# Order of the first transfers, index loads on GpSimd's queue, and products of zeros ahead of the first data

## Chip, core and metric

The kernel runs on one core of one Trainium2 chip. The metric is device time in microseconds; the time before is the median of three runs. A profile is one execution, with its own time.

## The reference

There are 1024 tokens of 512 features (8 batches of 128) in fp32, and two layers.

- Layer 0: `x + ffn0(cond0(x))`. `cond0` is a gated feed-forward part, `down(silu(gate(x)) * up(x))`, with 1376 hidden features, in which each of gate, up and down has a low-rank addition `0.5 * B_b (A_b x)` of rank 16. The pair `A_b`, `B_b` is chosen per batch by an index (`itok_B_2_6`). `ffn0` is a gated feed-forward part of 1792 hidden features with weights `w * (su @ sv)`, where `su @ sv` has rank 4.
- Layer 1: `x + ffn1(cond1(x))`. `cond1` is one 512x512 product with bias and a low-rank addition chosen by a second index; `ffn1` is a gated part with group-scaled integer weights.

Everything the change touches belongs to the start of `cond0`.

## The kernel before

Features lie on the 128 partitions and tokens along the free dimension. x is four tiles `x[0..3]` of 128 features by 1024 tokens, each loaded in two halves of 512 tokens (`load_x`, line 103; 256 KB a half). `cond0` runs over eleven units of 128 hidden features. Per unit there is one weight tile `wgu` (gate and up, 512 KB) and one `wd` (down, 256 KB).

Gate and up of a unit are not computed with eight block products but with seven (a Strassen-like scheme): product 1 takes the tokens' first half and features 0 to 255 ("11"), product 2 the features 256 to 511 of the first half ("21"), product 3 those of the second half ("22"), and products 4 to 7 take sums of blocks, `T1` to `T4` on the token side (`token_forms`, line 240, on VectorE) and `s` on the weight side (`weight_forms`, line 233). Each product is four matmuls of 128x128 by 128x512. In the first unit the order is 1, 3, 2, 6 (`T2`), 7 (`T3`), 5 (`T1`), 4 (`T4`) (`gate_up`, line 341). `T3` = second half of features 256 to 511 minus second half of 0 to 255, `T1` = second minus first half of features 0 to 255, and `T2` is made from `T1`, so all three need second halves of x.

The low-rank additions need the batch indices. `index_tiles` (line 92) loads them twice, spread over 128 partitions by 8 batches and as one number per partition; `row_indices` (line 111) turns them into row numbers, and GpSimd gathers rows of the A and B tables by them: `gather_b` one transfer (`gb`), `gather_a` eight (`ga`), of which five can be in flight, each copied into place by GpSimd (line 177). `arrange_b` (line 546) then copies `gb` inside the on-chip memory into `b_rows4` with eight DMAs. In the second unit, after its products 1, 6, 7 and 5, TensorE computes the low-rank products (`pt_gu`, line 554) and with `b_rows4` the additions of both units (line 574).

What sets the order: matmuls, and a part of the other operations, are kept in program order (`in_order`, line 68); the rest is placed by a scheduler when the program is built. A DMA waits on the queue of the engine that issues it (SP, ACT or GpSimd), so later issues on that queue, and for ACT and GpSimd also its computing, stand behind it. In the old kernel the index loads of layer 0 are first on ACT's queue (line 99), then x0 to x3, first halves; on SP's queue are w0 in two parts of 256 KB (line 273), the second halves of x from x3 to x0, then layer 1's indices, w1, the first `wd`, `fs` (line 533, the rank-4 factors of `ffn0`), w2 to w4 and the copies for `b_rows4`.

PSUM is one pool of eight banks (`bank`, line 88) here.

Of the kernel before, what the change touches and what calls it, by code (L numbers as in the profile page):

```python
# [7 lines left out]
F32 = mybir.dt.float32  # L8
# [3 lines left out]
ALU = mybir.AluOpType  # L12

P = 128
# [4 lines left out]
G = 32  # L19
NG = P // G  # L20
TG = T // NG
H = 512
KC = H // P
# [6 lines left out]
RS = 4  # L30
CA = 2 * KC + NF0
B_WIDTH = 2 * F0P + H
AHEAD = 3
QBUFS = 10
LAG = 2


@with_exitstack
def kernel(
# [25 lines left out]
    nc = tc.nc  # L65

    nc_mm = nc.tensor.matmul
    in_order = tc.keep_in_program_order

    def mm(*args, **kwargs):  # L70
        in_order(nc_mm(*args, **kwargs))  # L71

    def pool(stack, name: str, side: str, bufs: int = 1):
        return stack.enter_context(
            tc.tile_pool(name=name, side=side, bufs=bufs, reuse_waits="tile")
        )

    const = pool(ctx, "const", "left")
    scales = pool(ctx, "scales", "left", 3)
# [8 lines left out]
    def bank(name: str):  # L88
        return psum.tile([P, TB], F32, tag="bank", name=name)


    def index_tiles(which: str, engine, idx: bass.AP, idx_rows: bass.AP):
        a = const.tile([P, NB], I32, tag=f"a_{which}", name=f"a_{which}")
        engine.dma_start(out=a, in_=idx.to_broadcast([P, NB]))
        b = const.tile([P, 1], I32, tag=f"b_{which}", name=f"b_{which}")
        engine.dma_start(out=b, in_=idx_rows)
        return a, b

    ix0 = index_tiles("0", nc.scalar, idx0, idx0_rows)

    x = [const.tile([P, T], F32, tag=f"x{k}", name=f"x{k}") for k in range(KC)]

    def load_x(engine, k: int, tb: int):
        engine.dma_start(out=x[k][:, bass.ts(tb, TB)], in_=xT[:, k, bass.ts(tb, TB)])
# [3 lines left out]
    rank = const.tile([P, 1], I32, tag="rank", name="rank")  # L108
    nc.vector.tensor_single_scalar(rank, partition[:, 0:1], R - 1, ALU.bitwise_and)

    def row_indices(which: str, ix):
        rows = []
        for name, of, times, plus in (("a", ix[0], P, partition), ("b", ix[1], R, rank)):
            to = const.tile(
                list(of.shape), I32, tag=f"{name}_rows_{which}", name=f"{name}_rows_{which}"
            )
            in_order(
                nc.vector.scalar_tensor_tensor(to, of, times, plus, op0=ALU.mult, op1=ALU.add)
            )
            rows.append(to)  # L120
        return rows

    a0_rows, b0_rows = row_indices("0", ix0)
    row_batch = const.tile([P, 1], I32, tag="row_batch", name="row_batch")
    nc.vector.tensor_single_scalar(row_batch, partition[:, 0:1], R * (NB // NTB - 1), ALU.bitwise_and)

# [135 lines left out]
    def product(ps, a, b, start: bool, stop: bool):  # L262
        for n, (w, src) in enumerate(zip(a, b)):
            mm(ps, w, src, start=start and n == 0, stop=stop and n == len(b) - 1)


    ready = {}

    def load_c(f: int):
        wgu = wgu_pool.tile([P, 2, KC, P], F32, tag="wgu", name=f"wgu_c{f}")  # L270
        if f == 0:
            for s in range(2):
                nc.sync.dma_start(out=wgu[:, s], in_=c_gu[f, :, s])
        else:
            nc.sync.dma_start(out=wgu, in_=c_gu[f])
        wd = wd_pool.tile([P, H], F32, tag="wd", name=f"wd_c{f}")
        ready["c", f] = wgu, wd
# [16 lines left out]
    def finish_c(f: int):  # L294
        gate_up_forms("c", f, nc.vector if f < 3 else nc.gpsimd)

    fs = const.tile([P, 3, H], F32, tag="fs", name="fs")

    def load_f(f: int):
        wgu = wgu_pool.tile([P, 2, KC, P], F32, tag="wgu", name=f"wgu_f{f}")  # L300
        nc.sync.dma_start(out=wgu, in_=f_gu[f])
        wd = wd_pool.tile([P, H], F32, tag="wd", name=f"wd_f{f}")
        nc.sync.dma_start(out=wd, in_=f_down[f])
        si = scales.tile([P, 3, P], F32, tag="si", name=f"si_{f}")
        for s in range(3):
            nc.sync.dma_start(out=si[s * G : s * G + RS, s], in_=f_si[f, :, s])
        ready["f", f] = wgu, wd, si

    def finish_f(f: int):
        wgu, wd, si = ready["f", f]  # L310

        pw = [bank(f"pw_{f}_{s}") for s in range(3)]
        for k in range(KC):
            for s in range(3):
                rows, ks = slice(s * G, s * G + RS), bass.ts(k, P)
                sv, su = fs[rows, s, ks], si[rows, s, :]
                mm(pw[s][:, ks], *((su, sv) if s == 2 else (sv, su)), start=True, stop=True)
        for s in range(2):
            nc.vector.tensor_tensor(
                wgu[:, s].rearrange("p k f -> p (k f)"),  # L320
                wgu[:, s].rearrange("p k f -> p (k f)"), pw[s], ALU.mult,
            )
        nc.vector.tensor_tensor(wd, wd, pw[2], ALU.mult)
        gate_up_forms("f", f, nc.gpsimd)

    units = [("c", f) for f in range(NF0)] + [("f", f) for f in range(NF)]
    load = {"c": load_c, "f": load_f}
    finish = {"c": finish_c, "f": finish_f}

# [11 lines left out]
    def gate_up(  # L341
        act_pool, temps, layer: str, f: int, b, adapters=None, first=False, last=False, between=None
    ):


        a = ready[layer, f][0]
        mul = (nc.vector if last else nc.gpsimd).tensor_tensor

        def temp(what: str):
            return temps.tile([P, TB], F32, tag=what, name=f"{what}_{layer}{f}", bufs=2)  # L350

        def new(i: int):
            return bank(f"p{i}_{layer}{f}")

        act = [act_pool.tile([P, TB], F32, tag="act", name=f"act_{layer}{f}_{tb}") for tb in range(2)]
        add = nc.vector.tensor_tensor
        done = adapters is None
        p1, u, v = temp("p1"), temp("u"), temp("v")
        ps = {}

        def of(i: int, src: str, stop: bool = True):
            ps[i] = new(i)
            product(ps[i], a[i], b[src], True, stop)
            return ps[i]

        nc.scalar.copy(p1, of(1, "11"))
        if first:
            of(3, "22", done)
            of(2, "21", done)
        add(u, of(6, "T2"), p1, ALU.add)  # L370
        add(v, of(7, "T3"), u, ALU.add)
        add(act[1], of(5, "T1"), v, ALU.add)
        add(u, ps[5], u, ALU.add)
        if between is not None:
            between()
        if not first:
            of(3, "22", done)
            of(2, "21", done)
        of(4, "T4", done)
        x2, x3, x4 = ps[2], ps[3], ps[4]  # L380

        def finish():
            if adapters is not None:
                x8 = new(8)
                adapters([[x2, x3], [x4, x8]], {(1, 1)})
            add(p1, x2, p1, ALU.add)
            nc.scalar.activation(p1, p1, AF.Silu)  # L387
            add(act[0], x4, v, ALU.add)
            mul(act[0], act[0], p1, ALU.mult)  # L389
            add(u, x3, u, ALU.add)  # L390
            nc.scalar.activation(u, u, AF.Silu)  # L391
            if adapters is not None:
                add(act[1], x8, act[1], ALU.add)
            mul(act[1], act[1], u, ALU.mult)  # L394

        for tb in range(NTB):
            acts[f, tb] = act[tb]
        return finish
# [112 lines left out]
    with ExitStack() as c_layer:  # L511
# [2 lines left out]
        xf, top = ExitStack(), ExitStack()  # L514
        x_forms = pool(xf, "x_forms", "left")
        temps = pool(top, "temps_c", "right")
        load_x(nc.scalar, 0, 0)
        load_c(0)
        for k in range(1, KC):
            load_x(nc.scalar, k, 0)  # L520
        for k in reversed(range(KC)):
            load_x(nc.sync, k, 1)
        finish_c(0)
        b_x = token_forms(x_forms, "x", x, True)
        b0 = gather_b(temps, "0", c_b, b0_rows, B_WIDTH)
        a0, a0_down = gather_a(temps, "0", c_a, a0_rows, [(temps, 2 * KC), (l0, NF0)], nc.gpsimd)
        b0_down = l0.tile([P, H], F32, tag="b0_down", name="b0_down")
        in_order(nc.gpsimd.tensor_copy(b0_down, b0[:, 2 * F0P :]))
        a1_rows, b1_rows = row_indices("1", index_tiles("1", nc.sync, idx1, idx1_rows))
        load_c(1)  # L530
        load_c_down(0)
        for s in range(3):
            nc.sync.dma_start(out=fs[s * G : s * G + RS, s], in_=f_s[:, s])
        load_c(2)
        finish_c(1)

# [109 lines left out]
    for sign in (1, -1):  # L646
        in_order(
            nc.gpsimd.affine_select(
                out=one, in_=one, pattern=[[-sign, P]], compare_op=ALU.is_ge,
# [38 lines left out]
    def load_q(f: int):  # L688
        wgu = l1.tile([P, 2, KC, P], F32R, tag="wgu_q", name=f"wgu_q{f}", bufs=QBUFS)
        nc.gpsimd.dma_start(out=wgu, in_=q_gu[f])  # L690
        wd = l1.tile([P, H], F32R, tag="wd_q", name=f"wd_q{f}", bufs=QBUFS)
        nc.gpsimd.dma_start(out=wd, in_=q_down[f])
        ready["q", f] = wgu, wd

    for f in range(QBUFS):
        load_q(f)
# [145 lines left out]
    for f in range(NF - 1):  # L842
        d = f - LAG
        if d > 0 and d - 1 + QBUFS < NF:
            load_q(d - 1 + QBUFS)
        gate_or_up(f, 0, 0)
# [41 lines left out]
    f = NF - 1  # L888
    for tb, at in enumerate(halves):
        d = f - LAG + tb  # L890
        for s in range(2):
# [131 lines left out]
```

## Time and profile before

| What | us |
|---|---|
| Median of three runs (731.67 to 737.83) | 733.24 |
| The profiled execution's own time | 732.24 |
| Its span, first to last instruction | 730.5 |
| TensorE busy (96% of the span) | 698.1 |
| GpSimd busy | 380.3 |
| VectorE busy | 364.8 |
| ScalarE busy | 152.4 |
| First matmul starts at | 8.35 |

Times in the profile count from the span's start. L71 is the one line that all matmuls of layer 0 go through (`mm`), so they are told apart by their tiles: `p_c` are the gate and up products of `cond0`, `pt_gu` the low-rank ones. PE is TensorE, PEld its weight loads, DVE VectorE, ACT ScalarE, POOL GpSimd; SPq, ACTq and POOLq are DMA issues of these engines. q1 is the queue of SP's DMAs, q10 of ACT's, q0 of GpSimd's.

### The profile page before, as it was taken

Reading aid. Unit: us, or ns where it says so; the run is one execution under the profiler, and the core shown is the slowest. Engines: PE = TensorE matmul, PEld = TensorE weight load, DVE = VectorE, ACT = ScalarE, POOL = GpSimd, SP = SyncE. Lnnn points to the kernel's source line nnn. Section 1 sums busy time; section 2 is a strip of 40 time slices with the busy share of each in tenths; the row PEclk is TensorE's granted clock in tenths of the full one; section 3 lists DMA queues with packets and bytes.
Section 4 is the critical chain, followed back from the end, with each engine's and each line's share of the span. In section 5 each row is a group of like instructions: output and inputs, shape, how many; then the busy total and the mean of one; then the engine's idle time right before and its main releaser. Section 6 shows DMA issues by size and latency. Waiting matters only on the chain.

```text
span 730.5 us, 6906 instructions
## 1 busy us (share of the span) xinstructions
PE 698.1 (96%) x2526; PEld 366.3 (50%) x2526; DVE 364.8 (50%) x478; ACT 152.4 (21%) x191; POOL 380.3 (52%) x353
## 2 busy tenths in 40 slices
PE   5999999999999999999999998799999899999993
PEld 2444444444344444444444443344436687788862
DVE  4544434434035555544545360423124798899974
ACT  1111101111000111111111110000014555656552
POOL 4543524437460253443443369851301798898885
PEclk9999999999999999999999999799999999999998
DMA  8951001110020221110200020000900130000003
GB/s 303 269 190 58 29 30 57 30 30 31 0 72 1 86 59 29 41 49 29 59 5 1 15 73 0 0 29 29 373 1 9 50 86 16 15 0 1 0 1 115
DMA packets 16341, 41.48 MB, mean 57 GB/s; under 512 B 2882, under 2 KB 3162, under 8 KB 16052
## 3 DMA queue, kind: packets, MB, share of 16 engines
q1 hardware_dynamic: 10548, 25.51, 11.3%
q0 software_dynamic: 4896, 14.49, 6.2%
q10 hardware_dynamic: 864, 1.05, 0.4%
q8 instruction: 20, 0.33, 0.2%
q14 instruction: 13, 0.11, 0.0%
HBM read 37.50 MB, written 2.10 MB: 54 GB/s over the span
## 4 chain that ended last, share of the span: by engine, by line
PE 77%; POOL 11%; DMA 5%; issue 3%; ACT 1%; DVE 1%; POOLq 0%; ACTq 0%; SPq 0%; DVEq 0%
PE p_f L71 22%; PE p_c L71 17%; PE d_c L71 10%; PE gu_q L757 9%; PE d_f L71 8%; PE d_q L757 4%; PE l L722 4%; POOL sum L772 3%; PE pw L71 2%; POOL x L772 2%; POOL act_lo L772 1%; DMA wgu_c<-in_c_gu_dram 1%; DMA b<-in_idx_rows_dram 1%; DMA b_rows<-gb 1%; DMA x<-in_xT_dram 1%
## 5 line engine op out<-in xcount | busy, mean ns | idle before, releaser
L766 DVE SCALAR_TENSOR_TENSOR sum<-gu_q,sg,sum 128x1024 f32<-128x1024 f32 (+1 forms) x75 | 90.6, 1211 | 22.6 <-ACT sum L763 18.7
L757 PE MATMUL gu_q<-h_hi,wgu_q 128*128 128x512 f32 x224 | 88.8, 396 | 3.0 <-ACT sum L763 2.0
L757 PE MATMUL gu_q<-h_lo,wgu_q 128*128 128x512 f32 x224 | 87.3, 390 | 0.0
L394 POOL TENSOR_TENSOR act_f<-act_f,u_f 128x512 f32<-128x512 f32 x13 | 16.5, 1271 | 79.2 <-ACT u_f L391 79.2
L772 POOL TENSOR_TENSOR sum<-sum,sum 128x1024 f32<-128x1024 f32 (+1 forms) x15 | 33.9, 2258 | 38.7 <-DVE sum L766 38.7
L71 PE MATMUL p_f<-h,wgu_f 128*128 128x512 f32 x112 | 53.9, 603 | 0.0
L766 DVE SCALAR_TENSOR_TENSOR x<-d_q,sd,x 128x1024 f32<-128x1024 f32 (+1 forms) x49 | 53.0, 1100 | 0.9 <-PE d_q L757 0.9
L71 PE MATMUL p_f<-T_h,s_f 128*128 128x512 f32 x112 | 52.6, 592 | 0.0
L71 PE MATMUL p_f<-T_h,wgu_f 128*128 128x512 f32 x112 | 52.6, 592 | 0.0
L71 PE MATMUL p_c<-x,wgu_c 128*128 128x512 f32 x88 | 44.2, 626 | 8.3 <-DMA x<-in_xT_dram 8.3
L763 ACT ACTIVATE sum<-gu_q,sg 128x1024 f32<-128x1024 f32 (+1 forms) x45 | 47.3, 1056 | 20.0 <-PE gu_q L757 20.0
L757 PEld LDWEIGHTS gu_q<-h_hi,wgu_q 128*128 128x128 f32 x224 | 42.0, 188 | 17.3 <-ACT sum L763 3.0
L389 POOL TENSOR_TENSOR act_c<-act_c,p_c 128x512 f32<-128x512 f32 x10 | 12.8, 1277 | 70.3 <-ACT p_c L387 70.3
L757 PE MATMUL d_q<-act_hi,wd_q 128*128 128x512 f32 x112 | 44.7, 399 | 2.9 <-ACT y L763 1.6
L71 PE MATMUL d_f<-act_f,ds_f 128*128 128x512 f32 x84 | 40.2, 632 | 6.7 <-POOL ds_f L238 6.7
L757 PEld LDWEIGHTS gu_q<-h_lo,wgu_q 128*128 128x128 f32 x224 | 42.1, 188 | 8.2
L757 PE MATMUL d_q<-act_lo,wd_q 128*128 128x512 f32 x112 | 43.8, 391 | 0.8 <-POOL act_lo L772 0.8
L772 POOL TENSOR_TENSOR act_lo<-sum,act_hi 128x1024 fp32r<-128x1024 f32 (+1 forms) x15 | 33.8, 2255 | 17.8 <-ACT act_hi L833 17.8
L71 PE MATMUL p_c<-T_x,wgu_c 128*128 128x512 f32 x88 | 41.3, 592 | 0.0
L71 PE MATMUL p_c<-T_x,s_c 128*128 128x512 f32 x88 | 41.3, 592 | 0.0
L772 POOL TENSOR_TENSOR x<-x,y 128x1024 f32<-128x1024 f32 (+1 forms) x19 | 36.6, 1940 | 0.0
L71 PE MATMUL d_f<-act_f,wd_f 128*128 128x512 f32 x84 | 36.4, 592 | 0.0
(163 smaller groups left out, 1119.3 us busy)
## 6 DMA issues: line engine op xcount, KB each, us to landing
wgu_f<-in_f_gu_dram SPq DMA_DIRECT2D x14, 512.0 KB
wgu_q<-in_q_gu_dram POOLq DMA_DIRECT2D x14, 512.0 KB, 6.0
wgu_c<-in_c_gu_dram SPq DMA_DIRECT2D x10, 512.0 KB
wd_f<-in_f_down_dram SPq DMA_DIRECT2D x14, 256.0 KB
wd_q<-in_q_down_dram POOLq DMA_DIRECT2D x14, 256.0 KB
wd_c<-in_c_down_dram SPq DMA_DIRECT2D x11, 256.0 KB
out_dram<-x SPq DMA_DIRECT2D x8, 256.0 KB
b_rows<-gb SPq DMA_DIRECT2D x8, 176.0 KB
```

The source lines that it names most:

```text
L71: in_order(nc_mm(*args, **kwargs))
L389: mul(act[0], act[0], p1, ALU.mult)
L394: mul(act[1], act[1], u, ALU.mult)
L722: nc.tensor.matmul(l_sums[o][:, tb], lw[:, k, bass.ts(o, P)], x[k][:, bass.ts(tb, TB)], start=(k == 0), stop=False,)
L757: nc.tensor.matmul(ps, w, part[:, at], start=(n == 0), stop=(n == len(src) - 1))
L763: in_order(nc.scalar.activation(to, ps, AF.Identity, scale=scale))
L766: nc.vector.scalar_tensor_tensor(to, ps, scale, plus, op0=ALU.mult, op1=ALU.add)
L772: in_order(nc.gpsimd.tensor_tensor(to, a, b, op))
```

## The change

- The loads of layer 0's indices go from ACT's queue to GpSimd's, and the row numbers are computed on GpSimd, each with two operations (multiply, add) instead of one on VectorE. Layer 1's stay on SP's queue and on VectorE, with two operations each.
- w0 is loaded in four parts of 128 KB. The parts of w0 and the eight halves of x are laid on the queues of SP and ACT in the order of the products: SP gets w0 gate first part, x1, w0 gate second part, w0 up in two parts, then the second halves of x3 and x1; ACT gets x0, x2, x3 and then the second halves of x2 and x0.
- In the first unit product 2 comes before product 3.
- `fs` becomes one tile of 128x512 instead of 128x3x512. It is set to zero by VectorE at the start, and TensorE multiplies these zeros by each other four times (`WARM`) into a bank that nobody reads. The rank-4 factors are loaded over it later, the three factors on different partitions; `si` is cut in the same way.

```diff
+WARM = 4
...
+    fs = const.tile([P, H], F32, tag="fs", name="fs")
...
-    ix0 = index_tiles("0", nc.scalar, idx0, idx0_rows)
+    in_order(nc.vector.memset(fs, 0.0))
+    warm_bank = bank("warm")
+    for _ in range(WARM):
+        mm(warm_bank, fs[:, :P], fs, start=True, stop=True)
+
+    ix0 = index_tiles("0", nc.gpsimd, idx0, idx0_rows)
...
-            in_order(
-                nc.vector.scalar_tensor_tensor(to, of, times, plus, op0=ALU.mult, op1=ALU.add)
-            )
+            in_order(engine.tensor_single_scalar(to, of, times, ALU.mult))
+            in_order(engine.tensor_tensor(to, to, plus if name == "a" else plus[:, 0:1], ALU.add))
...
-        if f == 0:
-            for s in range(2):
-                nc.sync.dma_start(out=wgu[:, s], in_=c_gu[f, :, s])
-        else:
+        if f:
             nc.sync.dma_start(out=wgu, in_=c_gu[f])
...
-        si = scales.tile([P, 3, P], F32, tag="si", name=f"si_{f}")
+        si = scales.tile([P, P], F32, tag="si", name=f"si_{f}")
         for s in range(3):
-            nc.sync.dma_start(out=si[s * G : s * G + RS, s], in_=f_si[f, :, s])
+            nc.sync.dma_start(out=si[s * G : s * G + RS], in_=f_si[f, :, s])
...
         if first:
+            of(2, "21", done)
             of(3, "22", done)
-            of(2, "21", done)
...
+        load_c(0)
+        w0 = ready["c", 0][0]
+
+        def load_w0(s: int, i: int):
+            ks = bass.ts(i, KC // 2)
+            nc.sync.dma_start(out=w0[:, s, ks], in_=c_gu[0, :, s, ks])
+
+        load_w0(0, 0)
         load_x(nc.scalar, 0, 0)
-        load_c(0)
-        for k in range(1, KC):
-            load_x(nc.scalar, k, 0)
-        for k in reversed(range(KC)):
-            load_x(nc.sync, k, 1)
+        load_x(nc.sync, 1, 0)
+        load_x(nc.scalar, 2, 0)
+        load_w0(0, 1)
+        load_x(nc.scalar, 3, 0)
+        load_w0(1, 0)
+        load_w0(1, 1)
+        load_x(nc.scalar, 2, 1)
+        load_x(nc.sync, 3, 1)
+        load_x(nc.scalar, 0, 1)
+        load_x(nc.sync, 1, 1)
```

## The prediction

> **What bounds the kernel now.** I read the page first. TensorE is busy 96% of the span, and in the 40 slices only the first, the layer change near 60% and the tail fall under nine tenths. The change touches only the first slices, so I went to the chain of waits, cut to the first 60 us (start us, length us, what):
>
> ```profile
> 1.73 6.48 DMA x<-in_xT_dram
> 8.23 0.33 SPq L94
> 8.60 9.57 DMA b<-in_idx_rows_dram
> 18.19 9.96 DMA wgu_c<-in_c_gu_dram
> 28.17 8.22 DMA b_rows<-gb
> 36.43 23.61 PE p_c L71 x81
> ```
>
> Until 36.4 us the chain is made of transfers alone, from the first x block to the last slice of `b_rows4`; TensorE comes into it only then, though it has worked since 8.35. TensorE in order of time (start us, us, what, count, idle before):
>
> ```profile
> 8.35 3.75 PE L71 MATMUL p_c<-x,wgu_c 128*128 128x512 f32 x4 [8.35 <-DMA x<-in_xT_dram]
> 11.89 2.39 PE L71 MATMUL p_c<-x,s_c 128*128 128x512 f32 x4
> 14.12 1.88 PE L71 MATMUL p_c<-x,wgu_c 128*128 128x512 f32 x4
> 15.83 1.88 PE L71 MATMUL p_c<-T_x,s_c 128*128 128x512 f32 x4
> ...
> 29.66 2.35 PE L71 MATMUL pt_gu<-x,ga 128*32 128x256 f32 x36
> 32.38 1.92 PE L71 MATMUL pt_gu<-x,ga 128*32 128x256 f32 x28 [0.36 <-POOL ga L177]
> 35.09 2.04 PE L71 MATMUL p_c<-t_gu,b_rows 32*128 32x256 f32 x16 [0.79 <-DVE t_gu L567]
> ```
>
> Three losses stand here. TensorE is idle for 8.35 us. Its first four products start 3.54 us apart in sum and the next four 2.23, where a set of four takes 1.72 later: 1.82 + 0.51 = 2.3 us too long. Then come 0.36 and 0.79 us, and the sixteen adapter products take 1.96 us up to the next start against 1.08 in later units: 0.9 us, in which the last slice of `b_rows4` lands. All together some 12.7 us; after 37 us TensorE runs on without a gap for 100 us, so what is gained or lost at this join is carried to the end.
>
> Why x is late is seen in the windows (window us, length; PE, PEld, DVE, ACT, POOL busy us; clock; DMA share; GB/s) and in the DMA queues from 2 to 4 us:
>
> ```profile
> 2.00:3.00 1.00, 0.00 (x0) 0.00 (x0) 0.00 (x0) 0.00 (x0) 0.00 (x0) 1.00 0.88 224
> 3.00:4.00 1.00, 0.00 (x0) 0.00 (x0) 0.00 (x0) 0.00 (x0) 0.00 (x0) 1.00 0.71 130
> 4.00:5.00 1.00, 0.00 (x0) 0.00 (x0) 0.23 (x2) 0.00 (x0) 0.00 (x0) 1.00 0.55 105
> 5.00:6.00 1.00, 0.00 (x0) 0.00 (x0) 0.00 (x0) 0.00 (x0) 0.00 (x0) 1.00 0.72 242
> 6.00:7.00 1.00, 0.00 (x0) 0.00 (x0) 0.09 (x2) 0.00 (x0) 0.00 (x0) 1.00 1.06 383
> ```
>
> ```profile
> q1 hardware_dynamic: 187, 0.35, 75.8%
> q10 hardware_dynamic: 155, 0.00, 3.9%
> ```
>
> ACT's queue (q10) moves 155 packets of almost no bytes, the index loads of line 99, before x0; SP's (q1) moves w0 meanwhile, but at a third of the later rate. From 6 to 40 us the DMA share is about 1.0: weights, two gathers and the `b_rows4` copies fill every engine. This is the stage's limit. The waits of 0 to 60 us agree (us, times, longest):
>
> ```profile
> POOL ga L177 <- DMA ga<-in_c_a_dram,a_rows: 8.0, 3, 4.0
> PEld p_c L71 <- DMA b_rows<-gb: 0.5, 1, 0.5
> ```
>
> **What the Trainium skill says.** "DMA: Bandwidth & Descriptors", section "Queues, rings and completion order": each DMA engine takes turns between the queues it has work for, a packet at a time. The 155 small packets beside 187 large ones agree: each small packet delays its own queue by one large one, so a tiny load on ACT holds x0 back for microseconds. The same page, "Issuing engines are not separate DMA queues": loads issued by SP, ACT and GpSimd share the same engines, and other issuers save only issue time. So moving index loads removes no DMA work of itself; the saturated 6 to 40 us agree. "Specifications" there: under 512 B a transfer is a read-modify-write; that the rate falls to 105 GB/s while the small packets run fits it, but does not prove it. "TensorE: Matmul & The Clock Gate", Part 1: after idling the array runs at half clock until some 3.4 us of activity. The first four products at 0.885 us each against 0.43 agree, although the granted-clock column says 1.00.
>
> **The change, part by part.**
>
> *Order of loads, indices off ACT.* x0 is now first on ACT, and a quarter of w0 (128 KB) first on SP. The nearest row is w0's first half (256 KB), first on SP in the old kernel: issued at 0.82, it released a waiting SP issue at 4.19. So x0 lands at about 4.2 to 5.0 instead of 8.2, and TensorE can start at about 4.6: 3.7 us sooner.
>
> *Zeros.* The memset (128x512 on VectorE; a two-input operation of that size takes 0.68, estimate 0.3 to 0.7) ends near 1.2 us. Four products at the slow 0.885 are 3.5 us, 1.2 to 4.7. They end about when x0 lands, so they cost 0 to 0.5 us of start and take back up to 2.3 us of slow clock. Both lie ahead of a later wait, so neither counts by itself (next step).
>
> *What is late next: T2.* Products 1, 2 and 3 (12 matmuls of 0.43) would be through at 4.7 + 5.2 = 9.9. Product 6 needs T2, five VectorE operations (3.1 us by their starts at 11.98 and 15.08) after the last x block. That block landed at 11.95. From 2 to 6 us the DMAs moved 0.22 + 0.13 + 0.11 + 0.24 = 0.70 MB; at the 0.39 MB/us of the following microseconds they would have moved 1.56, so 2.2 us of DMA time were lost there. If the new order wins back none, x ends where it did; if all, at 9.7. I take 10.5 (half, and less of the gathers' traffic beside x), so T2 at 13.6 instead of TensorE's 15.83: 2.2 us sooner. The split w0 adds 1 KB runs instead of 2 KB, some tenths at most of DMA time; x's bytes are the same.
>
> *The next join: gathers and `b_rows4`.* TensorE would reach `pt_gu` at 29.66 - 2.2 = 27.5, but its second half needs the last gathered block (POOL waited 4.0 us for it, to 32.0), and the adapters need the last `b_rows4` slice at 36.39. Both stand at the end of a full DMA stream; they come sooner only by the DMA time won back, 0 to 2.2 us, plus what a better order of SP's queue gives: w0's four parts, three x blocks, then idx1, w1, wd0, fs, w2 to w4 and the eight copies. SP reaches idx1's loads some half microsecond to one sooner, when x2 is in. I take 2.0 us won at this join: a little over half of the lost time, 1.3, and 0.7 from SP's earlier issues.
>
> *Indices on GpSimd.* Two issues at the 0.54 us of the `wgu_q` row, from about 0.9. The trace has no small load on this queue: by that row a load lands 3.9 to 7.5 us after issue, so the second lands at 5.3 to 9.0 (6.88 before). Four POOL operations (nearest: the 0.13 us iota) replace two VectorE ones and a handover of 0.3: a few tenths. The first gather then issues between 5.9 and 9.6, against 7.36. Behind the wait on POOL stand the nine gathers and nothing else. I take 7.5, no change; the ends are worth about -1.5 and +2.2 us at the join.
>
> *At nothing.* VectorE drops an early wait for indices; its weight forms wait for w0 anyway. Layer 1's indices take two more VectorE operations of 0.16 us, ahead of which it waited 1.16 us for data. Product 2 before 3 only suits the order of landing; T2 hides it. fs and si keep their DMAs and bytes; they now share columns on different partitions, as the `b_rows4` copies do, none of which waited for another. fs must wait for the zeros, done 6 us before its old issue at 10.7; without that cover SP's w2 to w4 would stand behind it. The zero bank is free long before eight are in use.
>
> Sum: 730.5 - 2.0 = 728.5 span; the profiled run had 732.24, 1.74 more, so 730.2; the median of the shown runs is 1.0 above that run: **731.2 us**.
>
> **Rivals.**
> *TensorE sets the pace (0.24).* The index packets were the whole loss, x lands by 9.3, T2 by 12.5 (3.3 us sooner), and gathers and copies come in time, so that 0.36, 0.79 and 0.9 go as well: 5.3 us, 727.9. For it: the rate of 105 GB/s beside the packets. Against it: DMA at 1.0 up to 40 us. Even with x early enough for T2 the ceiling is 3.7 + 2.3 + 2.0 = 8.0, 725.2.
> *Hidden (0.12).* The index loads slow the engines from whatever queue, the stream ends where it did, and TensorE only waits at `pt_gu` rather than before 8.35: 733.2. The zeros failing to raise the clock gives no other time, since 2.3 us are covered by the waits for T2 and `pt_gu`.
> *Slower (0.10).* GpSimd's small loads take turns with two busy queues and land at 9.0, the gathers start 2.2 us later and with them the last `ga` and the last copy: 733.2 + 2.2 = 735.4. It decides once the second index load lands later than about 7, plus whatever DMA time is won. One per cent would take 7.3 us, three times that delay.
> The forecast has the remaining 0.54.
>
> **Numbers.** The 8 in 10 run from the first rival to just beyond the slow one, with 1 us for the median: 727.0 to 735.3. The shown runs span 731.67 to 737.83, so 1% (725.9 to 740.6) is about what can be told from no change. Beyond it on the fast side lies only the ceiling, a part of the first rival, and effects on the order elsewhere: 0.11. Slower by over 1%: 0.04. Within: 0.85.
>
> **What would show it.** Right: first real product at 4.2 to 5.5; four slow zeros before it and sets of 1.72 us from the first or second set on; an idle gap ahead of T2 at 12.5 to 14; a gap before the second half of `pt_gu`; last copy at about 34.4; the stretches after 40 us unchanged. Wrong: DMA rate still near 110 GB/s from 3 to 5 us, the first gather after 8 us, the last copy later than 36.4, or other gaps of TensorE after 40 us.

## The result and the profile after

| What | us |
|---|---|
| Median before, measured beside it (731.34 to 738.82) | 734.04 |
| Median after (733.4 to 739.38) | 736.57 |
| Ratio after to before, 95% interval | 1.0034 [1.0020, 1.0048] |
| Profiled execution after / its span | 737.68 / 735.9 |

The kernel became slower by 2.5 us [1.5 to 3.5], where 2.0 us less had been forecast. The profiled spans differ by 5.4, but the profiled execution of before was 1.8 us under its own median and that of after 1.1 over, so 2.9 of the 5.4 belong to the two executions. What follows is read from one profiled execution of each kernel.

First the chain of waits of the kernel after, cut to the first 60 us (start us, length us, what):

```profile
1.36 5.11 DMA a<-in_idx_dram
...
8.59 1.29 POOL gb L157
...
10.18 9.93 DMA ga<-in_c_a_dram,a_rows
...
24.87 9.63 DMA ga<-in_c_a_dram,a_rows
...
34.90 3.57 PE pt_gu L72 x28
...
39.24 20.91 PE p_c L72 x85
```

x and `b_rows4` are gone from it. It now runs from the index loads through GpSimd's first gather and its last, into `pt_gu`. TensorE in order of time (start us, us, what, count, idle before). The counts are records of the trace: the four products of zeros (`WARM`) stand there as eight, so one fp32 product is two records. A product of a unit, four records, is therefore two matmuls (`product` goes over two blocks) and not four, as the part on the kernel before has it.

```profile
1.53 6.65 PE L72 MATMUL warm<-fs 128*128 128x512 f32 x8 [1.53 <-DVE fs L102]
8.02 3.60 PE L72 MATMUL p_c<-x,wgu_c 128*128 128x512 f32 x8
...
14.01 1.98 PE L72 MATMUL p_c<-T_x,s_c 128*128 128x512 f32 x4 [0.68 <-DVE T_x L263]
...
30.57 2.89 PE L72 MATMUL pt_gu<-x,ga 128*32 128x256 f32 x32 [2.00 <-POOL ga L184]
34.90 3.54 PE L72 MATMUL pt_gu<-x,ga 128*32 128x256 f32 x28 [1.45 <-POOL ga L184]
39.24 1.22 PE L72 MATMUL p_c<-t_gu,b_rows 32*128 32x256 f32 x16 [0.80 <-DVE t_gu L583]
40.38 1.98 PE L72 MATMUL p_c<-x,s_c 128*128 128x512 f32 x4
```

T2's product starts at 14.01 instead of 15.83, and TensorE reaches `pt_gu` at 27.94 instead of 29.66: it is ahead by 1.7 us. Then it waits 2.00 and 1.45 us for gathered blocks, and the last 28 records of `pt_gu`, which took 1.92 us before, take 3.54. The first set after the join starts at 40.38, against 37.05: 3.3 us behind. From there to the start of `d_f` (429.12 against 425.79) the distance stays 3.33; another 0.8 appears in `d_f` and about 1.3 after 560 us, where the granted clock of after is 0.96 for 40 us and that of before 1.00.

The windows of after show both ends of this (window us, length; PE, PEld, DVE, ACT, POOL busy us; clock; DMA share; GB/s), first from 4 to 6 us, then inside `pt_gu`:

```profile
4.00:5.00 1.00, 1.00 (x2) 0.34 (x1) 0.00 (x0) 0.00 (x0) 0.00 (x0) 1.00 1.00 386
5.00:6.00 1.00, 1.00 (x3) 0.37 (x2) 0.00 (x0) 0.00 (x0) 0.00 (x0) 1.00 1.04 240
```

```profile
32.00:34.00 2.00, 1.46 (x16) 0.36 (x8) 0.00 (x0) 0.00 (x0) 0.57 (x2) 0.50 1.01 198
34.00:36.00 2.00, 1.10 (x12) 0.59 (x16) 0.00 (x0) 0.00 (x0) 1.45 (x4) 0.50 1.02 341
```

The early loss of DMA rate is partly won back (386 GB/s where 105 stood). A part of it has only moved: when the index packets run on GpSimd's queue they take 49% of the engines' time from 5.3 to 5.8 us, and the rate falls to 126 GB/s between 5.4 and 5.8 us. The granted clock is 0.50 from 32 to 38 us, where before it was 1.00.

The rate of about 200 GB/s marks the `b_rows4` copies. In the packets of the two traces the last of their rows (5632 bytes each) ends at 34.07 instead of 35.30. So this stream ended 1.2 us sooner, where 2.0 had been forecast for the join. The last gathered block went the other way: its last packet ends at 33.10 instead of 30.99, 1.0 us ahead of the end of the copies where it had been 4.3. On GpSimd (the same columns as for TensorE), before and after:

```profile
17.12 0.56 POOL L177 COPY ga<-ga 128x128 f32<-128x128 f32 x2 [1.77 <-DMA ga<-in_c_a_dram,a_rows]
17.96 0.98 POOL L150 DMA_INDIRECT ga<-in_c_a_dram,a_rows  x1 [0.27 <-POOL ga L177]
...
32.03 0.57 POOL L177 COPY ga<-ga 128x128 f32<-128x128 f32 x2 [4.04 <-DMA ga<-in_c_a_dram,a_rows]
```

```profile
20.16 0.56 POOL L184 COPY ga<-ga 128x128 f32<-128x128 f32 x2 [3.48 <-DMA ga<-in_c_a_dram,a_rows]
21.00 0.97 POOL L157 DMA_INDIRECT ga<-in_c_a_dram,a_rows  x1 [0.27 <-POOL ga L184]
...
34.55 0.57 POOL L184 COPY ga<-ga 128x128 f32<-128x128 f32 x2 [1.59 <-DMA ga<-in_c_a_dram,a_rows]
```

The first copy out of a landing tile is at 20.16 (17.12 before), so gathers six to eight are issued at 21.00 to 24.87 (17.96 to 22.04 before), so that most of their traffic falls beside the `b_rows4` copies, which move from 23.35 on (23.68 before). The last block is copied at 34.55 (32.03 before). After the last `b_rows4` slice only the adapter products are left; after the last `ga` block come the last 28 records of `pt_gu`, `t_gu` on VectorE and the adapters. That is the 3.3 us: last copy +2.5, `pt_gu` at half clock +1.6, and no wait for `b_rows4` any more, -0.8.

### The profile page after: what moved, and what is told of

Same layout as the page of the kernel before. It is cut to its first block, busy times and chain, and to the rows that moved or that the text cites. A ratio compares the mean times of both kernels' runs of the same rounds, so it can differ in the third digit from the quotient of the medians.

```text
span 735.9 us, 6932 instructions
## 1 busy us (share of the span) xinstructions
PE 706.7 (96%) x2534; PEld 369.7 (50%) x2534; DVE 365.7 (50%) x479; ACT 152.5 (21%) x191; POOL 381.5 (52%) x359
## 4 chain that ended last, share of the span: by engine, by line
PE 81%; POOL 10%; DMA 4%; issue 2%; DVE 1%; ACT 1%; POOLq 0%; DVEq 0%; ACTq 0%
PE p_f L72 22%; PE p_c L72 17%; PE gu_q L773 11%; PE d_c L72 10%; PE d_f L72 8%; PE d_q L773 5%; PE l L738 4%; DMA ga<-in_c_a_dram,a_rows 3%; PE pw L72 2%; POOL sum L788 2%; POOL x L788 1%; POOL ga L157 1%; POOL act_lo L788 1%; DVE sum L782 1%; DMA a<-in_idx_dram 1%
## 5 line engine op out<-in xcount | busy, mean ns | idle before, releaser
L72 PE MATMUL p_c<-x,wgu_c 128*128 128x512 f32 x88 | 42.1, 603 | 0.0
```

## The experiments

My theory after the result was that the gathers start later (8.59 against 7.36) because the indices come late on GpSimd's queue. The rival on record for the first run was that SP's weights, issued sooner, crowd the gathers. A further suspect was the clock. That not the start of the gathers but the gap ahead of the sixth decides, since only five tiles exist, was taken up after the first four runs. All kernels below compute the whole reference.

### Indices back on ACT

```diff
-    ix0 = index_tiles("0", nc.gpsimd, idx0, idx0_rows)
+    ix0 = index_tiles("0", nc.scalar, idx0, idx0_rows)
...
-            in_order(engine.tensor_single_scalar(to, of, times, ALU.mult))
-            in_order(engine.tensor_tensor(to, to, plus if name == "a" else plus[:, 0:1], ALU.add))
+            in_order(
+                nc.vector.scalar_tensor_tensor(to, of, times, plus, op0=ALU.mult, op1=ALU.add)
+            )
```

> The changed kernel with one part undone: layer 0's index loads go first on ACT's queue again and one VectorE operation each makes the row numbers. Theory (late gathers): the first gather is back at about 7.4 us instead of 8.59, the last ga block's copy at about 32 instead of 34.55, no stretch of half clock in pt_gu, first adapters at about 35 instead of 39.24; time 2.5 to 4 us under the changed kernel, level with the kernel before or up to 1.5 us under it. Rival (order of the loads): SP's weights, issued sooner than before, crowd the gathers whatever queue the indices use; last copy still after 33.5 and time within 1 us of the changed kernel.

736.2 us, ratio 1.0025 [1.0011, 1.0039]: not distinguishable from after. The gathers began at 5.51, 3 us sooner than in after. From 8 to 15 us GpSimd's queue then took 66% of the engines' time, and the last x block came at 15.6 instead of 10.8. ACT's packets of x also began 1.7 us later (3.84 against 2.16), behind the index packets; how much of the delay each of the two made is not separated. On TensorE:

```profile
18.43 3.78 PE L72 MATMUL p_c<-T_x,s_c 128*128 128x512 f32 x4 [5.59 <-DVE T_x L264]
```

TensorE waited 5.59 us for T2, with the set after it at half clock, and reached `pt_gu` only at 34.90; by then all blocks were there (last copy at 32.72). The same end by another way: neither theory had this. Here the earlier start of the gathers gained nothing, since x paid for it.

### Indices on GpSimd alone, in the kernel before

```diff
-    ix0 = index_tiles("0", nc.scalar, idx0, idx0_rows)
+    ix0 = index_tiles("0", nc.gpsimd, idx0, idx0_rows)
...
-    a0_rows, b0_rows = row_indices("0", ix0)
+    a0_rows, b0_rows = row_indices("0", ix0, nc.gpsimd)
```

(and the two operations per index, as in the change)

> The kernel before with one part alone: layer 0's index loads on GpSimd's queue and the row numbers made there by two operations each. Theory (late gathers): first gather at about 8.6, last ga copy 1.2 to 2.5 us later than 32.03, time 1 to 3 us above the kernel before. Rival (zeros or order of loads are to blame): within 0.7 us of the kernel before. A second rival: x0 is first on ACT now, lands near 5 and TensorE starts near 5, so it could also be faster by up to 1 us.

739.91 us, ratio 1.0077 [1.0046, 1.0108]: the index move alone costs 5.7 us, where 1 to 3 had been expected. GpSimd's gather and TensorE's wait:

```profile
10.38 1.07 POOL L149 DMA_INDIRECT gb<-in_c_b_dram,b_rows  x1 [0.35 <-POOL b_rows L118]
```

```profile
5.04 2.07 PE L71 MATMUL p_c<-x,wgu_c 128*128 128x512 f32 x2 [5.04 <-DMA x<-in_xT_dram]
...
35.19 3.42 PE L71 MATMUL pt_gu<-x,ga 128*32 128x256 f32 x32 [4.27 <-POOL ga L176]
```

Here the second index load was issued at 2.06 and used at 9.53, so the gathers begin 3 us late and the last block is copied at 38.45 (32.03 before). x0 is there at 5.04 without any other edit: taking the loads off ACT is what releases it. So the step is harmful through the gathers, and the rest of the change takes about half of the harm back.

### No products of zeros

```diff
-    warm_bank = bank("warm")
-    for _ in range(WARM):
-        mm(warm_bank, fs[:, :P], fs, start=True, stop=True)
```

> The changed kernel without the products of zeros (fs is still set to zero). Theory (late gathers): the first real product starts near 5 us, at half clock for about five matmul records; T2 starts near 14 as with the zeros, since T2 sets it; the last ga copy stays near 34.5 and the time within 0.7 us of the changed kernel. Rival (zeros in the way): the eight records of zeros that ran until 8.18 us held up the start, and without them the time falls by 1 us or more.

735.58 us, ratio 1.0022 [0.9999, 1.0045]: no measurable difference from after. On TensorE:

```profile
4.64 5.81 PE L71 MATMUL p_c<-x,wgu_c 128*128 128x512 f32 x8 [4.64 <-DMA x<-in_xT_dram]
...
14.44 2.53 PE L71 MATMUL p_c<-T_x,s_c 128*128 128x512 f32 x4 [1.91 <-DVE T_x L259]
...
34.10 1.92 PE L71 MATMUL pt_gu<-x,ga 128*32 128x256 f32 x28 [1.68 <-POOL ga L180]
```

x0 is used at 4.64, 3.4 us before TensorE was through with its zeros in after, where x0 is loaded in the same way. It makes no difference, since T2 sets the next start (14.44, and 14.01 with zeros). TensorE reaches `pt_gu` at 30.07, waits only once, for 1.68 us, and keeps its clock: the set after the join starts at 37.96, 2.4 sooner than in after (of which 0.8 from an earlier last copy, 33.76). So in these two profiles arriving sooner with zeros led only to longer waits and the half clock. The medians are 1.0 us apart, and the intervals of the ratios overlap.

### Zeros inside the waits of `pt_gu`

```diff
+    zeros = const.tile([P, H], F32, tag="zeros", name="zeros")
...
+                        if k == 0 and tb == 1:
+                            for _ in range(2):
+                                mm(fill, zeros[:, :P], zeros, start=True, stop=True)
```

In the first form the tile was cleared by VectorE just before the x forms:

> The changed kernel with two products of zeros (fp32, 128x128 by 128x512, into a bank that nobody reads) added before each of the two waits for gathered blocks inside pt_gu. Theory: the half clock from 32 to 38 us costs about 1.6 us (28 records of pt_gu in 3.54 us instead of 1.92); filling the two gaps of 2.0 and 1.45 us keeps the clock full, so the first adapters come 1.2 to 1.8 us sooner and the time falls by as much. Rival: narrow products do not count as activity, the clock falls all the same, and the zeros only add up to 0.5 us.

737.28 us, ratio 1.0044 [1.0028, 1.0060]. The clock stayed at full (28 records in 1.92 us), but this run says little on its question: the clearing shifted VectorE's other early work, so that GpSimd waited 5.44 us more and the gathers began at 14.56, 6 us later than in after. What it shows by accident is that the last block was then copied at 35.37, only 0.8 us later. So the start of the gathers does not carry through to their end by its own amount. In the second form the tile is cleared right behind `fs`:

> As the earlier run with zeros in the gaps of pt_gu, but the second zero tile is set right behind fs, so that no index step on VectorE moves and the first gather starts at 8.6 as in the changed kernel. Theory: pt_gu's last 28 records in 1.9 us instead of 3.54, adapters 1.2 to 1.8 us sooner than 39.24 (if the last ga copy stays at 34.5), time 1 to 1.8 us under the changed kernel. Rival: less than 0.5 us.

```profile
34.49 1.92 PE L72 MATMUL pt_gu<-x,ga 128*32 128x256 f32 x28
```

736.18 us, ratio 1.0021 [1.0009, 1.0034]. The clock is full, the last 28 records take 1.92 instead of 3.54, and the set after the join starts at 38.28, 2.1 sooner than in after (of which 0.9 from an earlier last copy, 33.61). In the ratios about 1 us of it is left, with intervals that overlap. So filling the gaps removes the half clock at the join, but what that is worth in the total is not shown; it is at most a second cause.

### Eight landing tiles

The gap ahead of the sixth gather, tested directly: with eight tiles no gather waits for a copy, and all eight can stand ahead of the `b_rows4` copies.

```diff
-        chunks, slots = sum(n for _, n in parts), 5
+        chunks, slots = sum(n for _, n in parts), NB
```

In the kernel after:

> The changed kernel with eight landing tiles instead of five for the gathered A blocks, so that gathers 6 to 8 no longer wait for copies and are issued by about 20 us, before most of the b_rows4 copies. Theory (the last gathers share the engines with the copies, packet by packet, and end with them): last ga copy before 30 us instead of 34.55, no wait inside pt_gu beyond 0.5 us, no half clock, adapters at 33 to 36 instead of 39.24, time 3 to 5 us under the changed kernel. Rival (only the amount of DMA work counts, not its order): last copy still within 1 us of 34.5 and the time within 1 us of the changed kernel.

In the kernel before (with `fs` and `si` cut to one tile, as in the change, to have the room):

> The kernel before with the same eight landing tiles; fs and si are cut to one 512- and one 128-column tile as in the change, without which the eight do not fit. Theory: here the last b_rows4 slice (36.39 us), not the last ga copy (32.03), ends the join, so earlier gathers bring at most 0.5 us. Rival (gathers bound both kernels): 1.5 us or more are won.

After with eight tiles: 722.64 us, ratio 0.9849 [0.9832, 0.9867]. The gathers are issued at 10.32 to 19.18, only 0.14 us apart from after in their start, and the last block is copied at 26.08 instead of 34.55. On GpSimd, and on TensorE, where no wait is left in `pt_gu`:

```profile
19.18 0.95 POOL L157 DMA_INDIRECT ga<-in_c_a_dram,a_rows  x1 [0.30 <-issue]
...
26.08 0.57 POOL L184 COPY ga<-ga 128x128 f32<-128x128 f32 x2 [0.89 <-DMA ga<-in_c_a_dram,a_rows]
```

```profile
28.89 3.66 PE L72 MATMUL pt_gu<-x,ga 128*32 128x256 f32 x64
33.36 1.69 PE L72 MATMUL p_c<-t_gu,b_rows 32*128 32x256 f32 x16 [0.81 <-DVE t_gu L583]
```

The set after the join starts at 34.98: 5.4 us sooner than in after, 2.1 sooner than before, at full clock. So in the kernel after, the gap ahead of the sixth gather was what turned a late start into a late end.

But the total fell by 13.6 us, well over twice that, and before with eight tiles gave 725.31 us, ratio 0.9868 [0.9835, 0.9900], although its join hardly moved:

```profile
36.59 3.78 PE L71 MATMUL p_c<-x,s_c 128*128 128x512 f32 x4
40.16 2.98 PE L71 MATMUL p_c<-x,wgu_c 128*128 128x512 f32 x4
```

The set after it starts 0.46 us sooner (36.59 against 37.05), but it and the next run at half clock, and `d_f` starts at 428.17 against 425.79. I had overlooked that `gather_a` has a second call, for layer 1. The last two runs follow from this; the one before them, on SP's queue, had been planned together with the eight tiles.

### The copies ahead of w3, w4 and the second `wd`

In the kernel with eight tiles, SP issues the `b_rows4` copies before these three loads, which are kept in program order for it.

```diff
         for f in range(NF0):
+            if not f:
+                arrange_b()
             prepare("c", f)
             if f:
                 load_c_down(f)
-            else:
-                arrange_b()
```

> The eight landing tiles in the changed kernel, and also w3, w4 and the second wd (1.25 MB, about 3.2 us at 0.39 MB/us) issued on SP behind the eight b_rows4 copies instead of ahead of them. Theory (a full DMA stream sets the join, so what stands ahead in it counts): last slice of b_rows4 1 to 3 us sooner than with the eight tiles alone, adapters at 31.5 to 34, time 1 to 2.5 us under that run. Rival (the copies wait for gb and gain nothing): within 0.5 us of it; or slower, if w3's weight forms come late.

721.97 us, ratio 0.9831 [0.9811, 0.9851]; against 0.9849 above this is no measurable difference. The copies' last packet ends at 29.94 instead of 33.19, although the scheduler also put eight small `si` loads ahead of them; but only 0.3 us of wait for `b_rows4` had been left with eight tiles, so there was little to win. In exchange the sets behind T2 took 2.63 and 2.97 us instead of 1.9, after a wait of 1.92.

### Eight tiles for one layer at a time

In the kernel after for layer 0 only:

```diff
-        chunks, slots = sum(n for _, n in parts), 5
+        chunks, slots = sum(n for _, n in parts), NB if name == "0" else 5
```

> The kernel after, with eight landing tiles instead of five for the A rows of layer 0 alone; layer 1's gather keeps its five. My theory: the two gains of the kernel with eight tiles in both layers are separate. This one keeps the join's 5 us (last copy of ga near 26, adapters near 33.4, next set near 35.0, full clock) and loses the 9 us of layer 1's d_f stage, whose wait of POOL for DVE's copy (about 3.3 us) comes back: 736.6 - 5.4 = 731.2, ratio to the kernel before near 0.996 (0.994 to 0.998). Rival: the join's gain is taken up by a later stage, as a half-clock phase or a wait, and the whole gain of eight tiles is that of layer 1: ratio 1.000 to 1.004.

In the kernel before for layer 1 only (`5 if name == "0" else NB`):

> The kernel before, with eight landing tiles for the A rows of layer 1 alone. My theory: the wait of POOL's queue for DVE's copy ahead of the weight forms ds_f is what TensorE waits for in d_f (6.7 us) and what lets the clock fall there, so the start stays as it was (adapters 35.1, next set near 37.05) and the d_f stage takes about 86 us instead of 95: ratio near 0.988 (0.985 to 0.991). Rival: the d_f stage was shortened by the start's other timing and not by the layer 1 gather: ratio 0.998 to 1.002, and d_f still near 95 us.

Layer 0 only: 732.85 us, ratio 0.9967 [0.9949, 0.9985]. Against after's 1.0034 that is 4.9 us less, with intervals apart, so the join's gain is kept to the end (`d_f` starts at 424.78, 4.3 us sooner than in after). The last copy was at 26.44; the set after the join started at 36.05, 1.1 later than expected, since TensorE waited 2.17 us for T2 and the set behind it took 3.49 us at half clock.

Layer 1 only: 724.63 us, ratio 0.9864 [0.9835, 0.9893]. What it removes is seen in the kernel before, first on GpSimd, then on TensorE:

```profile
430.64 1.16 POOL L150 DMA_INDIRECT ga<-in_l_a_dram,a_rows  x1 [3.33 <-DVE ga L177]
```

```profile
455.37 1.12 PE L71 MATMUL d_f<-act_f,ds_f 128*128 128x512 f32 x2 [1.95 <-POOL ds_f L238]
459.32 2.07 PE L71 MATMUL d_f<-act_f,ds_f 128*128 128x512 f32 x2 [2.82 <-POOL ds_f L238]
463.27 8.91 PE L71 MATMUL d_f<-act_f,ds_f 128*128 128x512 f32 x16 [1.88 <-POOL ds_f L238]
```

and with eight tiles in layer 1:

```profile
455.80 7.13 PE L71 MATMUL d_f<-act_f,ds_f 128*128 128x512 f32 x16 [0.97 <-POOL ds_f L238]
```

GpSimd's sixth gather of layer 1 waits 3.33 us for a copy on VectorE, and behind it on GpSimd's queue stand the weight forms `ds_f` that TensorE needs: it waits 6.65 us in three pieces, and the granted clock is 0.50 from 458 to 466 us. With eight tiles one wait of 0.97 us is left. From its start, `d_f` takes 86.9 us instead of 95.9. The start of the kernel is untouched (next set at 36.75).

The two gains agree with being separate: 0.9967 times 0.9864 is 0.9831, where both together gave 0.9849, and 0.9831 with the copies moved, which the intervals allow. Eight tiles in layer 0 gave the kernel before nothing that can be measured (0.9868 against 0.9864, a difference known to some 3 us), while they gave the kernel after 4.9 us. This is the evidence that the ring of five tiles is what makes the changed order lose.

The changed kernel with eight tiles in layer 0 stands 2.4 us [1.1 to 3.7] under the kernel before with five. How much of this is the change's own stays open: with eight tiles in both layers the two kernels have 0.9849 and 0.9868, 1.4 us apart with intervals that overlap. And of the 1.5% [1.3 to 1.7] that the changed kernel with eight tiles in both layers stands under before, nearly all can be had in the kernel before with eight tiles in layer 1 alone (0.9864 [0.9835, 0.9893]); the two are not told apart.

## Why the prediction was wrong

The sum gave 731.2 with a range up to 735.3; the ratio, put on the 733.24 it started from, gives 735.7.

- *Order of loads: right in the main.* x0 can be used at 4.64 without zeros (forecast 4.2 to 5.0). From 2 to 6 us the DMAs moved 0.161 + 0.226 + 0.386 + 0.240 = 1.01 MB instead of 0.70: 0.8 of the 2.2 us of lost DMA time were won back (1.1 forecast; the "third of the later rate" of the old queue holds from 3 to 5 us, while its mean from 2 to 4 us, 177 GB/s, is nearer to half). The last x block needed for T2 landed at 10.8 (10.5), T2's product started at 14.01 (13.6), `pt_gu` at 27.94 (27.5).
- *"Four products at the slow 0.885 are 3.5 us, 1.2 to 4.7": wrong by a factor of two.* The 0.885 us is the price of a record. A product of this size is two records, so four are eight of them, 6.65 us, and the first real product starts at 8.02 instead of 4.6. This step costs nothing by itself, as the run without zeros shows, since the wait for T2 covers it.
- *"I take 7.5, no change": the first step that failed.* The trace gives the first gather at 8.59, inside the range I had kept (5.9 to 9.6) but 1.1 later than the value. The second index load landed at 7.7, 5.6 us after its issue. Its price, up to 2.2 us at the join, takes the delay of the start for that of the end. The runs show otherwise: 1.2 us later in after moved the last copy by 2.5 us, and 3.0 us later in the kernel before with only the indices moved by 6.4. From after, 6 us more moved it by 0.8, and 3 us less by 1.8.
- *"Both stand at the end of a full DMA stream; they come sooner only by the DMA time won back": the step that decided.* I treated the last `ga` block and the last `b_rows4` slice as one join, 2.0 us sooner. The copies ended 1.2 us sooner, but the last `ga` block was copied 2.5 us later: the order in the stream had changed, from 4.3 us between the two ends to 1.0. And the `ga` block has work behind it that the slice doesn't have (the last 28 records of `pt_gu`, and `t_gu`: 3.1 us from the last copy to the adapters before, 4.7 in after). I had quoted "five can be in flight" and the 4.0 us wait for a block, and had not asked when the sixth gather could be issued.
- *Not foreseen: the clock.* TensorE's waits in `pt_gu` grew from 0.36 to 2.00 and 1.45 us, and the clock fell for 7 us: 1.6 us at the join in this profile. With zeros in the gaps it stayed at 1.00.
- *The slower rival (735.4)* had the first half of the mechanism: GpSimd's loads land late, "later than about 7", and the last `ga` follows. The second load landed at 7.7. But it let the last copy of `b_rows4` come later too, which came sooner, took the delay of the end to be that of the start, and had neither the gap ahead of the sixth gather nor the clock. That its 735.4 lies near 735.7 is luck. With a chance of 0.10 I had priced it too low: its condition lay well inside the range of 5.3 to 9.0 that I had worked out myself.
- *Hidden* and *TensorE sets the pace* fell. The latter had x by 9.3 and T2 by 12.5, and they came at 10.8 and 14.01; the index packets were not the whole loss, for in after the trace has none of them before 5 us, and the windows from 2 to 4 us still show 161 and 226 GB/s. *Hidden* is right in a part: the index packets cost DMA time on GpSimd's queue too, but the copies ended sooner all the same.

## What to carry to other kernels

At a join of two streams, follow each to its last byte and add what has to be done behind it; the one with more work behind it has to end first, and "the stream ends sooner" says nothing on that. Where a ring of landing tiles is smaller than the number of transfers, the price of a delay is not the delay, but where the first transfer that needs a used tile then falls in the traffic. And look at every caller of a helper: the larger gain lay in the second use of the same ring, where the waiting gather held up unrelated work on its engine's queue.

## What the hardware showed that I had not expected

- After gaps of 2.00 and 1.45 us with short narrow products between them the granted clock was 0.50 for about 7 us; after a gap of 2.17 us ahead of T2 it was so for some 3 us. Gaps of 1.44 to 1.92 us ahead of T2 cost the next sets between 0 and 1.7 us together (1.90 us cost nothing in one run, 1.91 us cost 1.7 in another). In the kernel before with eight tiles the clock fell for 7 us after gaps of only 0.81 and 0.39 us between narrow products. So the length of a single gap doesn't decide it, and what does is not shown. The Trainium skill, "TensorE: Matmul & The Clock Gate", section "Why this matters for your kernels", advises against gaps of more than some 3 us; here less was enough, so the measurement decides. Products of zeros put into the gaps kept the clock at 1.00.
- Small loads on GpSimd's queue landed 5.1 and 5.6 us after their issue in after, and the second was used 7.5 us after its issue in the kernel before with only the indices moved. The Trainium skill, "DMA: Bandwidth & Descriptors", section "Anatomy of one DMA — SWDGE (gpsimd) path", has about 2 us as the fixed part. In after, the trace has no packet of that queue before 5 us, so most of the time passed before the data moved; why is not shown.
- The copies inside the on-chip memory ran at about 200 GB/s with the DMA share at 1.0, half of what the loads reached (403 to 415 from 14 to 20 us in after), and gathered blocks beside them were copied into place 2.2 us apart. This agrees with the late end of a gather that falls beside them.
